# Filling TensorE's gaps at the start of a fused FFN, attention and FFN kernel, and reordering its first transfers and copies

## The chip, the cores and the metric

The kernel runs on one core of one Trainium2 chip. The time is the device time of the whole program in microseconds (us). The kernel before the change took 918.1 us, the median of three runs (916.91 to 918.52).

## The reference, cut to what matters

x has 8 batches of 512 rows of 256 numbers, all in fp32. The two FFNs share their weights. Their butterflies are linear maps of 1,024 features in 10 stages, where stage s pairs features 2^s apart.

```python
def _L0_ffn_ref(x, W_exp, b_exp, up_weights, up_bias, down_weights, W_con, b_con, down_bias):
    h = jnp.einsum('bsd,dh->bsh', x, W_exp) + b_exp
    h = butterfly(h, up_weights, D_HIDDEN)
    h = jax.nn.gelu(h + up_bias, approximate=False)
    h = butterfly(h, down_weights, D_HIDDEN)
    y = jnp.einsum('bsh,hd->bsd', h, W_con) + b_con
    return y + down_bias
...
x = x + 0.5 * ffn(layernorm(x))
x = x + attention(layernorm(x))   # causal, 16 heads, 32 numbers per head
x = x + 0.5 * ffn(layernorm(x))
```

## The kernel before, in words

Everything between x and the gelu is linear, and so is everything behind it, so the kernel first folds each butterfly into a dense matrix: W_exp and the up butterfly become `wup_sb` (256 x 1,024), W_con and the down butterfly become `wdn_sb`. This folding is the prologue, and it is where the change lies. After it, all eight batches run through FFN, attention and FFN with plain matrix products, in an order written out by hand (the `ORDER` strings), one token per step. There the engines' queues are fixed.

The prologue, in the order in which it is written (from L572):

- SyncE's queue issues the large loads: the up butterfly's tables `upe_sb` in two pieces (L117, L118), W_exp in two halves of 4 blocks (L120), the first x (`load_x(0)`, L106), the tables of the down butterfly, W_con, the second x, the attention weights, two more x. ScalarE's queue issues five small ones (L121 to L125), among them `upc_sb`, the coefficients of the high stages, and the two biases.
- GpSimd makes the identity (`ident`), the causal mask and constants.
- `low_matrices` (L208, VectorE) multiplies the tables of the seven low stages into one 128 x 128 matrix for each of the 8 blocks of 128 features. VectorE then adds the two output biases and halves them (`bhalf`).
- `low_up` (L237, TensorE) multiplies W_exp with these matrices: eight products of 128 x 257, into eight PSUM banks: four of the tile `low_up`, three of pool `ps_a` (`low_up_0` to `_2`), one of `ps_o`. Pool `ps_a` has three banks in all, and all later tiles `pxt`, `pup`, `ph`, `low_dn` turn in it.
- `ln_stats` and `ln_apply` normalize the first x. The statistics are VectorE's (L152 to L154), the rstd GpSimd's (L156). For this first x GpSimd also does the normalization (L167), and behind each half of it the addition of `bhalf` to x (L172), which is the residual with the biases already in it. VectorE does the normalization of all other x.
- Three high stages (`high_stage`, L221 and L226) combine blocks that are 1, 2 and 4 apart. For each block ScalarE scales it (`mine`), and VectorE adds the partner, scaled. The first stage reads PSUM, the other two read SBUF.
- Behind the second stage, the normalized x is transposed by TensorE (L180, `pxt`, four transposes for each half of the 256 columns) and copied from PSUM by VectorE (L181).
- `finish_up` transposes the result of the third stage (L246, `pup`, 16 transposes in four quarters), copied to `wup_sb` by ScalarE and VectorE in turn (L247). GpSimd adds the bias column (L241).
- Layer one of the first x follows on TensorE (L271, `ph`, then gelu on ScalarE, L278), three of its eight steps between each two high stages of the down butterfly (`high_dn`), then `low_down` (L252) makes `wdn_sb`, and layer two follows (L289, `py`).

An fp32 product of TensorE stands in the trace as two records, each with its own weight load; a transpose stands as one.

## Time and profile before

| what | value |
|---|---|
| median of 3 runs | 918.1 us (916.91 to 918.52) |
| the profiled execution | 918.08 us |
| its span, first to last instruction | 916.3 us |
| mean granted TensorE clock | 0.987 |
| TensorE busy | 880.8 us (96%) |
| VectorE busy | 634.1 us (69%) |
| ScalarE busy | 495.9 us (54%) |
| GpSimd busy | 87.5 us (10%) |

The span is what the trace shows; 1.8 us of the profiled execution lie outside it. Times within it count from its first instruction. PE is TensorE, PEld its weight loads, DVE VectorE, ACT ScalarE, POOL GpSimd, SP SyncE. The end of a TensorE record is modelled, so where records follow closely, the distance between their starts says what one costs. The granted clock is the share of the full clock that TensorE is given.

In the first 30 us the large transfers land one after the other, each about 1.4 us after the one before: the first half of W_exp at 9.58, the second at 10.98, the first x at 12.43, the last x at 27.46.

### The profile page before, as it was taken

What the parts mean: (1) busy time and instruction counts of PE and PEld (TensorE: products, weight loads), DVE (VectorE), ACT (ScalarE), POOL (GpSimd) and SP (SyncE); (2) the same over time, 40 slices, a digit from 0 to 9 for tenths busy, and PEclk for the clock granted to TensorE, in tenths of its full rate; (3) what the DMA queues carried; (4) which work ended last, traced back from release to release, by engine and by line L of the source; (5) the groups of instructions that cost most, each with busy time, mean ns of one, the idle gap of its engine ahead of it and who ended that gap; (6) DMA issues with size and microseconds to landing.
All of it is one profiled execution on the core that took longest, in us unless ns stands there. A gap on an engine that the chain in (4) does not pass through costs nothing.

```text
span 916.3 us, 13349 instructions
## 1 busy us (share of the span) xinstructions
PE 880.8 (96%) x4464; PEld 516.3 (56%) x4464; DVE 634.1 (69%) x1772; ACT 495.9 (54%) x1336; POOL 87.5 (10%) x103
## 2 busy tenths in 40 slices
PE   3999999999999999999999999999999999998988
PEld 2474654666547465564746655465655554743746
DVE  5854986898619985399826987189767886987230
ACT  4615677646537455554736465356558367558111
POOL 4321000022000210012000220002100200010010
PEclk9799999999999999999999999999999999999989
DMA  9100555555651356542572555604554565665500
GB/s 328 52 1 1 127 127 127 127 127 127 150 149 41 88 138 161 127 118 63 137 181 56 127 126 127 172 18 110 139 146 120 133 152 144 160 175 145 150 1 23
DMA packets 37812, 108.14 MB, mean 118 GB/s; under 512 B 9200, under 2 KB 20208, under 8 KB 37744
## 3 DMA queue, kind: packets, MB, share of 16 engines
q1 hardware_dynamic: 37024, 106.98, 45.8%
q8 instruction: 35, 0.57, 0.3%
q10 hardware_dynamic: 720, 0.32, 0.1%
q14 instruction: 33, 0.27, 0.1%
HBM read 10.79 MB, written 4.19 MB: 16 GB/s over the span
## 4 chain that ended last, share of the span: by engine, by line
PE 92%; DVE 4%; DMA 1%; POOL 1%; issue 1%; ACT 1%; DVEq 0%; SPq 0%; POOLq 0%; ACTq 0%
PE ph_f L271 25%; PE py_f L289 25%; PE pp L314 12%; PE sc L364 10%; PE po L465 6%; PE pv L328 6%; PE pa L444 5%; DVE e L378 3%; PE pxt_f L180 2%; PE pxt_at L180 1%; DMA x<-in_x_dram 1%; POOL xn_f L167 1%; DMA upc_sb<-in_up_c_dram 0%; PE pup L246 0%; ACT e L391 0%
## 5 line engine op out<-in xcount | busy, mean ns | idle before, releaser
L391 ACT ACTIVATE e<-e,nm 128x128 f32<-128x128 f32 (+3 forms) x512 | 280.2, 549 | 108.9 <-DVE nm L378 108.3
L378 DVE CUSTOM_DVE_ANT_0 e<-sc,mask 128x128 f32<-128x128 f32 (+3 forms) x512 | 216.3, 486 | 124.8 <-PE sc L364 124.7
L271 PE MATMUL ph_f<-xnt_f,wup_sb 128*128 128x512 f32 x512 | 234.6, 605 | 0.0
L289 PE MATMUL py_f<-wdn_sb,g_f 128*128 128x256 f32 x1024 | 233.2, 382 | 0.0
L289 PEld LDWEIGHTS py_f<-wdn_sb,g_f 128*128 128x128 f32 x1024 | 191.3, 190 | 35.3 <-issue 6.5
L409 DVE STREAM_TRANSPOSE pr<-e 128x1536 f32<-128x1536 f32 (+2 forms) x128 | 170.7, 1356 | 5.8 <-ACT e L391 5.8
L278 ACT ACTIVATE g_f<-ph_f,bup_sb 128x512 f32<-128x512 f32 x128 | 86.5, 686 | 150.7 <-PE ph_f L271 150.4
L271 PEld LDWEIGHTS ph_f<-xnt_f,wup_sb 128*128 128x128 f32 x512 | 97.4, 194 | 117.3 <-issue 106.9
L364 PE MATMUL sc<-kt,qt 32*128 32x128 f32 (+3 forms) x1024 | 91.9, 461 | 10.0 <-DVE nm L378 8.1
L391 ACT ACTIVATION_READ_ACCUMULATOR e<-e,nm 128x1 f32 x512 | 95.8, 187 | 0.0
L156 POOL TENSOR_TENSOR rstd_f<-mv_f,mhalf 128x2 f32<-128x2 f32 x32 | 22.5, 704 | 633.7 <-DVE mv_f L154 630.6
L444 PE MATMUL pa<-pt,v 128*32 128x512 f32 (+3 forms) x1024 | 75.5, 436 | 0.3 <-issue 0.2
L364 PEld LDWEIGHTS sc<-kt,qt 32*128 32x128 f32 x1024 | 44.6, 184 | 51.2 <-issue 21.5
L444 PEld LDWEIGHTS pa<-pt,v 128*32 128x32 f32 x1024 | 30.4, 110 | 60.0 <-issue 53.7
L314 PE MATMUL pp<-xnt_at,wq_sb 128*128 128x512 f32 x128 | 61.5, 603 | 0.0
L314 PE MATMUL pp<-xnt_at,wk_sb 128*128 128x512 f32 x128 | 60.7, 596 | 0.0
L465 PE MATMUL po<-wo_sb,ot 128*128 128x256 f32 x256 | 58.8, 382 | 0.0
L328 PE MATMUL pv<-wv_sb,xnt_at 128*128 128x512 f32 x128 | 57.7, 595 | 0.0
L451 DVE TENSOR_TENSOR ot<-pa,pt 128x512 f32<-128x512 f32 x32 | 21.8, 681 | 51.3 <-PE pa L444 50.3
L298 DVE SCALAR_TENSOR_TENSOR x<-py_f,x 128x512 f32<-128x512 f32 x32 | 21.7, 678 | 49.4 <-PE py_f L289 49.4
L465 PEld LDWEIGHTS po<-wo_sb,ot 128*128 128x128 f32 x256 | 48.1, 190 | 9.0 <-issue 2.2
L172 POOL TENSOR_TENSOR x<-x,bhalf 128x512 f32<-128x512 f32 x32 | 40.9, 1279 | 32.9 <-DVE xn_f L167 32.2
(69 smaller groups left out, 578.1 us busy)
## 6 DMA issues: line engine op xcount, KB each, us to landing
pt<-pr SPq DMA_DIRECT2D x512, 176.0 KB, 4.0
x<-in_x_dram SPq DMA_DIRECT2D x8, 512.0 KB, 5.5
out_dram<-x SPq DMA_DIRECT2D x16, 256.0 KB, 3.8
wexp_sb<-in_wexp_t_dram SPq DMA_DIRECT2D x2, 514.0 KB, 6.9
wcon_sb<-in_wcon_dram SPq DMA_DIRECT2D x1, 1024.0 KB, 9.1
dne_sb<-in_dn_e_dram SPq DMA_DIRECT2D x1, 1016.0 KB, 7.2
upe_sb<-in_up_e_dram SPq DMA_DIRECT2D x1, 512.0 KB, 6.3
wq_sb<-in_wq_dram SPq DMA_DIRECT2D x1, 512.0 KB, 10.4
```

The lines of the kernel that those rows point to most:

```text
L172: nc.gpsimd.tensor_tensor(x2, x2, bhalf.rearrange("p (o c) -> p o c", o=1).to_broadcast([P, 2, C]), ALU.add)
L271: nc.tensor.matmul(ph[:, :N], lhsT=wup_sb[:, kc, bass.ts(fc, P)], rhs=xnt[:, kc, :], start=(kc == 0), stop=(kc == KC - 1),)
L278: nc.scalar.activation(g[:, fc, :], ph[:, :N], AF.Gelu, bias=bup_sb[:, fc : fc + 1])
L289: nc.tensor.matmul(py[:, i, :], lhsT=g[:, fc, bass.ts(t, P)], rhs=wdn_sb[:, fc, :], start=(fc == 0), stop=(fc == NBLK - 1),)
L314: nc.tensor.matmul(pp[:, :N], lhsT=w[:, kc, bass.ts(g, P)], rhs=xnt[:, kc, :], start=(kc == 0), stop=(kc == KC - 1))
L328: nc.tensor.matmul(pp, lhsT=xnt[:, kc, bass.ts(t, P)], rhs=wv_sb[:, kc, :], start=(kc == 0), stop=(kc == KC - 1))
L364: nc.tensor.matmul(sc[:, j, at : at + n], lhsT=kept["q", b, gg][r, bass.ts(qb, P)], rhs=kept["k", b, gg][r, :n], start=(i == 0), stop=True ...
L378: nc.vector.tensor_tensor_reduce(out=e[:, j, at : at + n], in0=sc[:, j, at : at + n], in1=mask[:, N - n :], scale=-1.0, scalar=3.0e38, op0 ...
L391: nc.scalar.activation(e[:, j, at : at + n], e[:, j, at : at + n], AF.Exp, scale=-1.0, bias=nm[:, qb, gg, j : j + 1], accum_out=zs[:, gg, ...
L409: nc.vector.transpose(pr[:, :, :, qb : qb + 3 * n - 2 : 3, :].rearrange("p j h k r -> p h k j r"), blocks[:, :, :n])
L444: nc.tensor.matmul(by_row[r, :, kb * 32 :], lhsT=v[:, kb, bass.ds(g * P + j * HD, HD)], rhs=pt[:, :, bass.ds(j * NSLOT + SLOT[kb] + kb, NT ...
L465: nc.tensor.matmul(po[:, i, :], lhsT=ot[:, g, bass.ts(t, P)], rhs=wo_sb[:, g, :], start=(g == 0), stop=(g == NG - 1))
```

## The change

- `load_x(0)` is issued between the two halves of W_exp and no longer behind both.
- For the normalization on GpSimd (the first x alone) the two additions of `bhalf` are no longer done behind each half; they are a function of their own, `ffn_bias`, called behind the high stages. On GpSimd's queue they come directly behind the four normalizations.
- The transposes of the first normalized x and their copies move from behind the second high stage to behind the third, and the copies from VectorE to ScalarE.
- A new function, `keep_busy`, multiplies the identity with itself into a PSUM tile that nothing reads: 50 times at the very start, in the bank that `low_up_o` gets later, and 12 times between the transposes of x and those of W_up, in bank 6 of `ps_a`.

In the built program's queues, TensorE has the 50 products, then the eight of `low_up`, eight transposes of x, the 12 products, and from there the order of before. The banks of `pxt`, `pup` and `ph` stay the same; the first quarter's `pup` takes over the bank of the 12 products, and the second and third take those of `pxt`, which ScalarE's copies free. VectorE's queue loses the two copies, and ScalarE's has them between its last `mine` of the third stage and the first copy of `pup`.

```diff
     for blocks in (slice(0, NBLK // 2), slice(NBLK // 2, NBLK)):
         nc.sync.dma_start(out=wexp_sb[:, blocks, :], in_=wexp_t.rearrange("(n p) c -> p n c", p=P)[:, blocks, :])
+        if blocks.start == 0:
+            load_x(0)
...
-    load_x(0)
     nc.sync.dma_start(out=dne_sb, in_=dn_e)
...
-        if what != "at":
-
-            nc.gpsimd.tensor_tensor(
-                x2, x2, bhalf.rearrange("p (o c) -> p o c", o=1).to_broadcast([P, 2, C]), ALU.add
-            )
-
-    def transposed(b, what, xn, xnt, kc):
+        if what != "at" and engine is nc.vector:
+            ffn_bias(b, half)
+
+    def ffn_bias(b, half):
+
+        x2 = xt[b][:, 2 * half : 2 * half + 2, :]
+        nc.gpsimd.tensor_tensor(x2, x2, bhalf.rearrange("p (o c) -> p o c", o=1).to_broadcast([P, 2, C]), ALU.add)
+
+    def transposed(b, what, xn, xnt, kc, copy=nc.vector.tensor_copy):
...
-        nc.vector.tensor_copy(xnt[:, kc, :], pt[:, :N])
+        copy(xnt[:, kc, :], pt[:, :N])
...
+    def keep_busy(pool, tag, times):
+
+        idle = pool.tile([P, 512], F32, name=f"idle_{times}", tag=tag)
+        for _ in range(times):
+            nc.tensor.matmul(idle[:, :P], lhsT=ident, rhs=ident, start=True, stop=True)
+
...
     with fold, tc.manual_schedule():
+        keep_busy(ps_o, "pa", 50)
         mats = low_matrices(upe_sb, "up")
...
         for i in range(HIGH):
             cur, whole = high_stage(cur, i, upc_sb, "up", C + 1, NBLK)
-            if i == 1:
-                run(ln_steps(0, "f1"))
+        run(ln_steps(0, "f1", copy=nc.scalar.copy), partial(ffn_bias, 0, 0), partial(ffn_bias, 0, 1))
+        keep_busy(ps_a, "a", 12)
         finish_up(cur, whole)
```

## The prediction

> **What bounds the kernel now.** I read the page first, then the chain of waits for the first 75 us, then the timelines of TensorE and VectorE there, then the windows of the clock. On the page TensorE is busy in 96% of the span, and its idle slices lie at both ends:

> ```profile
> PE   3999999999999999999999999999999999998988
> PEclk9799999999999999999999999999999999999989
> ```

> One slice is 22.9 us. The change touches only the first two. From 30.2 us on TensorE is dense up to 821 us, in a written order, so whatever moves the first product of layer one (L271, 30.20) or its clock moves the end by as much; nothing else here can. The chain of waits in order of time (start, length, what):

> ```profile
> 5.48 6.95 DMA x<-in_x_dram
> ...
> 15.88 2.41 POOL xn_f L167 x2
> 18.37 1.51 POOL x L172
> 19.88 3.75 POOL xn_f L167 x2
> ...
> 23.67 1.34 PE pxt_f L180 x5
> ...
> 25.65 0.49 DVE high_up L226
> ...
> 26.18 4.22 PE pup L246 x16
> 30.40 14.89 PE ph_f L271 x32
> ```

> First x lands at 12.43; GpSimd normalizes it, with a bias addition in between; TensorE transposes it; VectorE copies it and only then does its last high stage. VectorE's timeline shows the price of that place (start, length, count, idle before):

> ```profile
> 18.27 4.42 DVE L226 SCALAR_TENSOR_TENSOR high_up<-high_up,upc_sb,mine_up 128x257 f32<-128x257 f32 x8
> 24.19 0.69 DVE L181 COPY xnt_f<-pxt_f 128x512 f32<-128x512 f32 x1 [1.50 <-PE pxt_f L180]
> 25.04 0.69 DVE L181 COPY xnt_f<-pxt_f 128x512 f32<-128x512 f32 x1 [0.16 <-PE pxt_f L180]
> 25.65 3.25 DVE L226 SCALAR_TENSOR_TENSOR high_up<-high_up,upc_sb,mine_up 128x257 f32<-128x257 f32 x8
> ```

> The second stage ends at 22.69, the third starts at 25.65: 2.96 us of waits and copies. The second stage itself takes 4.42 for eight, the third 3.25: one of its instructions lasts 1.50 instead of 0.48, beside GpSimd's bias addition (18.37, 1.51).

> The clock needs two views. TensorE's timeline:

> ```profile
> 9.72 6.14 PE L237 MATMUL low_up<-wexp_sb,mat_up 128*128 128x257 f32 x14 [9.72 <-DMA wexp_sb<-in_wexp_t_dram]
> 15.69 0.60 PE L237 MATMUL low_up_o<-wexp_sb,mat_up 128*128 128x257 f32 x2
> ```

> Fourteen records in 6.14 us start 0.43 us apart; the last two, 0.22. So the clock was at half speed until about 15.5, though the granted-clock column shows 1.00 there: it knows nothing before its first event. From then on it can be read (window, length, PE, PEld, DVE, ACT, POOL, clock, DMA):

> ```profile
> 15.53:18.94 3.41, 1.39 (x6) 0.61 (x4) 3.41 (x10) 3.34 (x9) 3.33 (x4) 1.00 1.08 393
> ...
> 25.77:29.18 3.41, 3.00 (x12) 2.34 (x13) 3.41 (x9) 0.59 (x1) 0.20 (x1) 0.50 0.16 52
> 29.18:32.60 3.42, 3.42 (x9) 2.03 (x8) 2.34 (x7) 3.01 (x8) 0.00 (x1) 0.50 0.00 0
> 32.60:36.01 3.41, 3.41 (x9) 1.52 (x8) 3.38 (x7) 3.32 (x5) 0.00 (x0) 1.00 0.02 5
> 824.48:827.90 3.42, 1.80 (x18) 0.80 (x11) 3.12 (x8) 2.06 (x9) 0.00 (x0) 1.00 0.58 138
> 838.14:841.55 3.41, 1.16 (x17) 0.81 (x17) 2.19 (x8) 2.96 (x6) 0.00 (x0) 1.00 0.99 264
> ```

> All changes lie on one grid of 3.41 us. A window with 1.39 or 1.16 us of TensorE work is followed by half clock, one with 1.80 is not; a window full of work is followed by full clock. Half clock costs layer one (32.6 - 30.2) / 2 = 1.2 us today.

> **The change, part by part.** All times below are of the profiled execution (918.08 us, 1.8 outside its span); it stands at the median of the runs, 918.1.

> *Fifty products of the identity.* They begin when GpSimd has made it (1.61), say at 1.8. Each fp32 product is two records (the fp32 products of L289 are 1024 records for 512). The trace has no 128-column ordinary stream, so from both sides: by columns, L289's 256-column record every 0.216 us gives 0.108; the 128-column transposes start 0.11 apart at full and 0.21 at half clock (L246); weight loads of 128 columns start 0.11 apart at best (82.67 and 82.78). Above, one load is recorded as 0.19, which would hold only if loads were not hidden, and beside L289 they are. I take 0.109 and 0.214: 10.9 us at full speed, 21.4 at half. When does the clock rise? The rows say 5.8 us after dense work began (9.7 to 15.5) and 6.4 (26.2 to 32.6, with gaps at first). [...] Half-speed records by then: (6.9 - 1.8) / 0.214 = 24; the other 76 take 8.3; the fifty end at 15.2 (14.4 to 16.0).

> That is late. low_up stands behind them on TensorE, and began at 9.72. Now it begins at 15.2, at full clock: its first four blocks, eight records, are done 1.9 us later instead of 3.7; ScalarE's first product (13.52 before) starts at 17.1, and VectorE's first stage 0.45 later, 17.6 instead of 15.13. It loses 2.45 us.

> *x between the halves of W_exp.* The two transfers swap: x lands at 10.98, the second half at 12.43 instead of 10.98 (both have 0.5 MB, queues are full). Statistics end 1.4 us earlier, at 13.7. This gains nothing while low_up ends them later; the swapped half is hidden by the fifty, and would cost up to 1 us without them, as blocks 4 to 7 would wait to 12.4. The transfers after them keep their places on SP; ScalarE's queue is not touched.

> *Biases behind, copies to ScalarE.* GpSimd runs rstd, then four normalizations without the addition: 14.5 + 4 x 1.21 = 19.3 instead of 23.6, beside a first stage that reads PSUM and did not slow it before. The additions follow at 19.3 and 20.6, to 21.9, and meet the second stage, which starts about 20.7; the sum for bup_sb behind them on GpSimd waits for the third stage anyway. Cost as seen: 1.0 (0.3 to 1.2), against 1.25 before. VectorE loses both copies and their waits: 2.96 gained. ScalarE's 24 products end 0.55 after the second stage, at 25.4, and it idled 4.6 us there; two copies of 0.59 end at 26.6, well before layer one. Behind them in its queue stand the W_up copies, and the transposes of the second and third quarter wait for the banks that the copies free (26.0 and 26.6): they are due at 26.6 and 27.0, so nothing.

> Sum for the end of the third stage: 28.90 + 2.45 - 2.96 - 0.2 = 28.2 (27.1 to 28.2 over the phases, since an early rise brings low_up forward). TensorE then needs 1.2 us of transposes at half clock, or 0.75, the copy of the second quarter, at full clock. Layer one starts at 28.3 to 29.3 instead of 30.20: 1.3 us, on the mean.

> *Twelve products.* The transposes of x run at 19.4 to 20.3, the twelve (24 records, 2.6 us) wait for bank 6, free after the first stage (20.6), and end at 23.2; behind them stand the W_up transposes, not due before 25.3. The first W_up transpose comes at 25.3, and until 28 they come at VectorE's pace, 0.4 us apart. So there is again a hole of 2.1 us and sparse work after it. With the grid at its four phases I get a window under 1.4 us of work, hence half clock, in about two of four; in the other two the clock survives and the 1.2 us are saved. Where it falls, a window of transposes and layer one must raise it. Rows: the window 29.18 to 32.60 was full, a third of it transposes, and did. [...] I take the row. Mean saving on the clock 0.6 to 0.7.

> Total: -1.3 - 0.65 = -1.9 us: 916.2. By phase the same sum runs from -2.7 to -1.2.

> **Rivals.**
> *A, the fifty end before W_exp is there*, if an identity product costs half of what I take. For: nothing but that the trace has no such row. Then low_up starts at 9.7, waits for the second half to 12.4, statistics decide (13.7), the third stage ends near 24.7, layer one starts at 25.5, warm: -4.7 - 1 = about 912.5.
> *B, slower: the identity stream does not raise the clock.* Place: in front of low_up. The fifty then take 21.4 us, to 23.2; low_up at half clock brings the first stage to 27.3, the third to 36.8, layer one to 38: +8, 926. Loss begins when the fifty end after 16.9 (28.9 - 11.9), which is a rise after 10.4 us. Against: low_up raised it within 5.8 us, and the stream is as dense; for: the operands are nearly all zeros, and no row has such.
> [...]

> **How the numbers follow.** My forecast 0.64, A 0.12, B 0.05, C 0.16, and 0.03 for a loss that I do not see. A difference under 0.2%, 1.8 us, cannot be told from none here. Of the forecast's phases some six in ten lie beyond -1.8 (0.39), the rest within. Faster: 0.39 + 0.12 = 0.51; same: 0.25 + 0.15 = 0.40; slower 0.09. The range takes in A's 912.5 and C with a bad phase, 919: 912.4 to 919.2; outside are B and the unseen loss.

> **What would show it.** The fifty ending at 14.4 to 16.0 and low_up's records 0.22 apart; ScalarE's first product near 17; no copy between the second and third stage, third stage ending at 27 to 28.2; layer one at 28.3 to 29.3; half clock, if at all, only between about 25.7 and 31. Wrong if the fifty end before 12 or after 17, if bias additions cost VectorE over 1.5 us, or if half clock lasts past 32.

## The result and the profile after

| | before | changed |
|---|---|---|
| median of 14 runs each | 918.12 us (916.74 to 921.70) | 918.13 us (916.34 to 921.16) |
| profiled execution, span | 918.08, 916.3 | 916.75, 915.0 |
| mean granted clock in it | 0.987 | 0.996 |

The ratio of the runs is 1.0001, 95% interval 0.9989 to 1.0013: no difference that can be measured. Yet the profiled execution is 1.3 us shorter, and its page shows what the change was meant to do: TensorE is busy from the start, and its clock row is full at both ends.

```profile
PE   8999999999999999999999999999999999998988
PEclk9999999999999999999999999999999999999999
```

To see where time went I cut each trace at two points that every kernel here has: the first product of layer two of the first batch, and the first score of the last batch. I call the three pieces head, middle and end.

| profile | layer one starts | head | middle | end | half clock at (number of 3.41 us windows) |
|---|---|---|---|---|---|
| before | 30.20 | 48.77 | 722.74 | 144.77 | 18.9 (4), 841.6 (1), 879.1 (2) |
| changed | 29.31 | 47.23 | 722.74 | 144.99 | 825.9 (1), 880.5 (1) |

The change gained 1.54 us in the head; the end took 0.22 longer, and the remaining 1.3 us is what this execution's span is shorter by. The chain of waits of the changed kernel (start, length, what) is a different one from before; x, GpSimd's normalization and the copies have left it:

```profile
1.67 13.82 PE idle L247 x100
15.49 1.76 PE low_up L240 x8
...
17.27 1.58 ACT mine_up L224 x4
...
18.88 1.50 DVE high_up L229 x4
...
25.39 3.27 DVE high_up L229 x8
...
28.70 0.34 PE pup L255
...
32.87 1.28 ACT L287
...
34.16 0.70 ACT g_f L287
...
34.90 8.85 PE ph_f L280 x20
```

Line by line: the hundred records of the identity now hold TensorE to 15.49, and `low_up` waits for them, not for W_exp. VectorE's first stage follows the *fourth* of ScalarE's products (17.27 + 1.58 = 18.85). The later stages run without a break. And a link appears that the prediction had not named: ScalarE's table load and first gelu, which stand in its queue behind eight products for the down butterfly (29.55 to 32.85), and on which layer one waits until 34.90. VectorE's timeline (start, length, count, idle before) shows that the copies are gone from between the stages, and that the second and third together now take 6.62 us:

```profile
18.88 2.44 DVE L229 SCALAR_TENSOR_TENSOR high_up<-low_up,upc_sb,mine_up 128x257 f32<-128x257 f32 x6 [5.03 <-ACT mine_up L224]
...
22.03 6.62 DVE L229 SCALAR_TENSOR_TENSOR high_up<-high_up,upc_sb,mine_up 128x257 f32<-128x257 f32 x16
28.57 0.68 DVE L256 COPY wup_sb<-pup 128x512 f32<-128x512 f32 x1
```

TensorE's timeline shows the twelve products between the transposes, those of W_up at full clock (3.45 us where before had 4.22), and the new wait:

```profile
22.16 2.94 PE L247 MATMUL idle<-ident 128*128 128x128 f32 x24
26.02 3.45 PE L255 MATMUL pup<-ident,high_up 128*128 128x128 f32 x16 [0.91 <-DVE high_up L229]
29.31 5.42 PE L280 MATMUL ph_f<-xnt_f,wup_sb 128*128 128x512 f32 x12
34.90 8.85 PE L280 MATMUL ph_f<-xnt_f,wup_sb 128*128 128x512 f32 x20 [0.18 <-ACT g_f L287]
```

So two questions are left. Is the head's gain what the prediction thought it was, and which part of the change makes it? And why do the medians not show it?

### The profile page after: what moved, and what is told of

Read it like the earlier page. It is cut to its first block, busy times and chain, and to the rows that moved or that the text cites. A ratio compares the mean times of both kernels' runs of the same rounds, so it can differ in the third digit from the quotient of the medians.

```text
span 915.0 us, 13597 instructions
## 1 busy us (share of the span) xinstructions
PE 890.5 (97%) x4588; PEld 527.2 (58%) x4588; DVE 632.1 (69%) x1770; ACT 496.6 (54%) x1338; POOL 85.8 (9%) x103
## 4 chain that ended last, share of the span: by engine, by line
PE 92%; DVE 5%; ACT 1%; issue 1%; DVEq 0%; POOL 0%; POOLq 0%
PE py_f L298 25%; PE ph_f L280 24%; PE pp L323 12%; PE sc L373 10%; PE po L474 6%; PE pv L337 6%; PE pa L453 5%; DVE e L387 3%; PE pxt_f L183 2%; PE idle L247 2%; DVE high_up L229 1%; PE pxt_at L183 1%; ACT e L400 0%; PE low_dn L261 0%; ACT mine_dn L224 0%
## 5 line engine op out<-in xcount | busy, mean ns | idle before, releaser
L307 DVE SCALAR_TENSOR_TENSOR x<-py_f,x 128x512 f32<-128x512 f32 x32 | 21.7, 678 | 48.4 <-PE py_f L298 48.4
```

## The experiments

Two theories on the head. The **queue theory**: the order of x, biases and copies gains, and the fifty take part of it back, because `low_up` stands behind them. Its rival: the fifty pay for themselves, through the full clock. Every kernel below computes everything that the reference does; only unread products are added or taken away, or the order changes. Each ratio is to runs of the kernel before on the same chip (35, 37 or 33 of them, with medians of 917.84, 917.48 and 917.65 us on the three chips used); it is taken over the runs and is not simply the quotient of the two medians. All times that are read off come from one profile each. The head of the changed kernel was 47.23, 47.36 and 47.26 in three profiles, and in these three the clock rose at nearly the same time, 6.7 to 7.0. Where the clock's phase differs, a head differs more: that of the kernel before took 48.77 in its own profile and 48.20 in that of the kernel with the end filled (below), with full clock from 32.6 and from 31.4. So a difference of less than some 0.6 us between two heads can be the phase alone.

### Fewer products at the start, none, and none at all

```diff
-        keep_busy(ps_o, "pa", 50)
+        keep_busy(ps_o, "pa", 20)
```

> The changed kernel with 20 instead of 50 products of the identity at the start. Queue theory (the fifty end at 15.5 and hold low_up back by 5.8 us; that eats the gain of the reordering): the twenty end by about 8.6, low_up starts at 9.6 to 9.8, VectorE's first stage starts at about 14 behind the statistics, not 18.9; the third stage ends near 25, layer one starts at 25.5 to 28; median 913 to 916. Rival, clock theory (when low_up starts does not matter; the time is made by how long the clock is at half speed, and a shorter stream loses it sooner): layer one starts no earlier than 29 and median 918 to 920.5.

Measured: a median of 918.31 us (916.49 to 920.64), ratio 1.0000 (0.9987 to 1.0012). `low_up` began at 9.95 at full clock and the third stage ended at 25.8, both as the queue theory has it. Layer one did not follow: it started at 29.63, past what was expected. TensorE's timeline says why:

```profile
22.46 5.23 PE L247 MATMUL idle<-ident 128*128 128x128 f32 x24
27.74 2.00 PE L255 MATMUL pup<-ident,high_up 128*128 128x128 f32 x16
29.63 14.38 PE L280 MATMUL ph_f<-xnt_f,wup_sb 128*128 128x512 f32 x32
```

The transposes of W_up were ready at 25.8, and the twelve products stood in front of them until 27.7. They were late because they come behind the transposes of x, whose normalization GpSimd did beside VectorE's second stage:

```profile
14.68 6.61 POOL L168 TENSOR_SCALAR xn_f<-x,mv_f,rstd_f 128x256 f32<-128x256 f32 x4
```

That is 6.61 us, against 4.83 for the same four in the changed kernel. And they were at half clock (5.23 us where they take 2.94 in the changed kernel), since TensorE had been nearly idle since 14.8. Products meant to keep the clock had become the wait.

The fifty left out, the twelve kept:

```diff
-        keep_busy(ps_o, "pa", 50)
```

> The changed kernel without the first 50 products, with the 12 later ones. Queue theory: low_up starts at 9.7 at half clock, VectorE's first stage at about 14, third stage ends near 25; but the twelve then run at half clock in most executions (24 records of 0.214, 5.1 us, from about 20) and stand in front of the transposes of W_up, so layer one starts at 26 to 29: median 914.5 to 917. Clock theory: as slow as the slowest runs of the changed kernel, 920 or more.

Measured: 918.54 us (915.19 to 920.37), ratio 0.9991 (0.9976 to 1.0007). Layer one at 27.90, head 45.84: 1.4 us better than with the fifty. But the runs fell into two groups, six from 915.2 to 915.7 and eight from 918.5 to 920.4, with nothing between. I come back to that.

Neither of them, only the order:

```diff
-        keep_busy(ps_o, "pa", 50)
...
-        keep_busy(ps_a, "a", 12)
```

> The changed kernel without any product of the identity: the earlier x, the additions behind and the copies on ScalarE alone. Queue theory: third stage ends near 25 against 28.8 before, layer one starts at about 26, at half clock until 29 to 31: median 913.5 to 915.5, so faster than the full change. Clock theory: no gain beyond what the whole change has, 917.5 to 919, since the clock is at half speed as long as before.

Measured: 917.21 us (915.49 to 920.25), ratio 0.9994 (0.9981 to 1.0007). Head 46.71: in the head the order alone gains 2.06 us, more than the whole change. (The medians of the two do not differ beyond the scatter of the runs.) VectorE's timeline:

```profile
15.07 2.45 DVE L229 SCALAR_TENSOR_TENSOR high_up<-low_up,upc_sb,mine_up 128x257 f32<-128x257 f32 x6 [1.32 <-ACT mine_up L224]
...
18.21 8.98 DVE L229 SCALAR_TENSOR_TENSOR high_up<-high_up,upc_sb,mine_up 128x257 f32<-128x257 f32 x16
```

The first stage is 3.81 us earlier than in the changed kernel (15.07 against 18.88), but the two stages after it take 8.98 instead of 6.62, because now they meet GpSimd's bias additions. Two of VectorE's sixteen instructions make nearly all of the difference: they start at 19.64 and 21.16 and take 1.60 and 1.48 us where the others take 0.48, and GpSimd's timeline has its two bias additions there:

```profile
19.68 2.68 POOL L177 TENSOR_TENSOR x<-x,bhalf 128x512 f32<-128x512 f32 x2
```

So of the 3.8 us that the fifty cost, 2.4 come back: they delay the stages past GpSimd's additions. In TensorE's timeline the transposes of W_up are at half clock again:

```profile
24.48 4.22 PE L255 MATMUL pup<-ident,high_up 128*128 128x128 f32 x16 [3.50 <-DVE high_up L229]
28.49 14.73 PE L280 MATMUL ph_f<-xnt_f,wup_sb 128*128 128x512 f32 x32
```

### The twelve left out, and the products alone

```diff
-        keep_busy(ps_a, "a", 12)
```

> The changed kernel without the 12 later products; the 50 stay. Third stage ends at 28.6 as with them. If the 12 keep the clock (the change's purpose), TensorE now idles from 22 to 26 and the clock falls in most executions: layer one at half speed for some us, first product of layer two at 48 to 49.5 instead of 47.2. If they are not needed or stand in the way, 47.2 as before.

Measured: 919.55 us (919.21 to 921.96), ratio 1.0027 (1.0018 to 1.0036). The clock fell from 24.1 to 30.9, and TensorE's timeline has the half-clock transposes again:

```profile
26.07 4.23 PE L255 MATMUL pup<-ident,high_up 128*128 128x128 f32 x16 [3.77 <-DVE high_up L229]
30.10 14.32 PE L280 MATMUL ph_f<-xnt_f,wup_sb 128*128 128x512 f32 x32
```

Head 47.89, 0.66 us more. `low_up` itself began 0.16 later here (15.48 against 15.32), so the twelve are worth about 0.5 us in the head of this profile: they hold the clock through the hole. The runs are slower by more than that; in the profile the rest lies in the end, which took 146.8 us (below).

The kernel before with all 62 products, each at the place that the change gives it (the twelve stand behind the third stage), and nothing else:

```diff
     with fold, tc.manual_schedule():
+        keep_busy(ps_o, "pa", 50)
...
+        keep_busy(ps_a, "a", 12)
         finish_up(cur, whole)
```

> The kernel before with only the products of the identity added (50 at the start, 12 in front of the transposes of W_up); x, additions and copies as before. Queue theory: low_up starts at 15.5 and VectorE's first stage at 18.9 instead of 15.13, third stage ends near 30 instead of 28.8 (the wait for x's normalization between the stages becomes shorter), layer one starts at 30.6 or later, at full clock if it survives: first product of layer two at 48.5 to 50 against 48.77 before, median 918 to 919.5. Clock theory: full clock saves its 1.2 us and more: first product of layer two at 47.5 or earlier.

Measured: 919.58 us (917.61 to 923.71), ratio 1.0021 (1.0011 to 1.0032): a small loss. The profile has a head of 48.30, 0.47 us under before, which can be the phase alone, and it is of the fastest of the 18 runs. The clock rose early in it, at 4.7 against 6.7 in the changed kernel, so that `low_up`, which is on this kernel's chain too, started at 14.38 and not at 15.3. With a later rise the gain would be gone (an estimate from this one profile); what the slower runs lost, and where, no profile shows. TensorE's timeline:

```profile
14.38 3.21 PE L237 MATMUL low_up<-wexp_sb,mat_up 128*128 128x257 f32 x14
...
23.10 3.85 PE L244 MATMUL idle<-ident 128*128 128x128 f32 x24
```

### Products where they hold nothing up

Twenty at the start, 26 between `low_up` and the transposes of x, and no twelve in front of W_up's:

```diff
-        keep_busy(ps_o, "pa", 50)
+        keep_busy(ps_o, "pa", 20)
...
+        keep_busy(ps_a, "a", 26)
         run(ln_steps(0, "f1", copy=nc.scalar.copy), partial(ffn_bias, 0, 0), partial(ffn_bias, 0, 1))
-        keep_busy(ps_a, "a", 12)
```

> The changed kernel with 20 products at the start, 26 between low_up and the transposes of x, and none between those and the transposes of W_up. Queue theory: TensorE's products then stand only in front of work that is not due. low_up starts near 9.9, VectorE's first stage at 13.8, third stage ends near 25.8 (as with 20 and 12); the 26 run from about 16 to 22 at full clock, the transposes of x behind them to 23; layer one starts at 26.3 to 27 at full clock, the first product of layer two at 44 to 45 (48.8 before, 47.2 changed). The end of the program adds its own scatter of up to 3.4 us; median 913 to 915.5. Rival (the clock alone sets the time, and it was already full in the changed kernel's profile): first product of layer two at 47, median as the changed kernel.

Measured: 917.05 us (913.93 to 918.91), ratio 0.9989 (0.9975 to 1.0003). TensorE's timeline:

```profile
9.78 1.98 PE L240 MATMUL low_up<-wexp_sb,mat_up 128*128 128x257 f32 x8 [0.64 <-DMA wexp_sb<-in_wexp_t_dram]
...
15.66 6.07 PE L247 MATMUL idle<-ident 128*128 128x128 f32 x52 [1.16 <-DVE high_up L229]
...
26.20 5.42 PE L280 MATMUL ph_f<-xnt_f,wup_sb 128*128 128x512 f32 x12
```

Head 44.13, at full clock from 7.5 us on: 4.64 us under before and 3.10 under the changed kernel. The queue theory stands. But the median moved by 0.4 us only, inside its interval. This can't be explained from the head of this profile.

### The end

All ten profiles up to here have the same middle, 722.72 to 722.80 us. What differs is the end: 144.8 to 145.05 in seven, 146.8 in one, 148.3 in two, and one of those two is the kernel with the shortest head. The clock windows of the profile without the fifty (window, length, PE, PEld, DVE, ACT, POOL, clock, DMA) show it:

```profile
825.42:828.84 3.42, 3.42 (x11) 0.68 (x13) 3.42 (x13) 3.42 (x15) 0.00 (x0) 0.50 0.00 0
839.08:842.50 3.42, 3.07 (x18) 1.76 (x19) 1.21 (x7) 3.02 (x9) 0.00 (x0) 0.50 1.03 237
842.50:845.90 3.40, 3.40 (x6) 1.33 (x5) 3.40 (x13) 3.40 (x15) 0.00 (x0) 0.50 0.70 167
880.05:883.46 3.41, 2.16 (x7) 1.61 (x8) 2.68 (x4) 0.00 (x0) 2.31 (x2) 0.50 0.00 0
```

The last batch has no other batch to fill in for it, so TensorE has gaps at about 820, 837 and 877 (in the changed kernel 1.05 and 1.92 us idle at the first, 2.65 at the second, 2.60 at the third). The windows lie on a grid of 3.41 us, and where it lies against the gaps differs between the profiles: a window begins 0.84 us behind the score that ends the first idle stretch here (822.00, 821.16), and 0.04 us ahead of the same score in the changed kernel (822.48, 822.52). The same view of the changed kernel, two windows and their successors:

```profile
822.48:825.90 3.42, 1.47 (x17) 0.73 (x18) 2.88 (x3) 2.61 (x11) 0.00 (x0) 1.00 0.78 183
825.90:829.31 3.41, 3.41 (x4) 0.98 (x4) 3.38 (x17) 2.85 (x11) 0.00 (x0) 0.50 0.02 5
836.14:839.55 3.41, 2.04 (x11) 0.45 (x9) 1.30 (x5) 1.21 (x2) 0.00 (x0) 1.00 0.94 263
839.55:842.96 3.41, 2.13 (x19) 1.29 (x20) 2.14 (x10) 3.40 (x8) 0.00 (x0) 1.00 1.03 240
```

The first has 1.47 us of TensorE work and is followed by half clock; the third has 2.04 and is not. (Where a row is at half clock its PE time is stretched, as the identity's records are, 0.213 us apart there and 0.111 at full clock, so only rows at 1.00 are compared.) In the kernel without the fifty the grid lay so that the window at the second gap, from 835.67, had only 1.10 us of work: half clock from 839.08 to 845.90, and after the third gap two windows of it instead of one. Its 148.35 us of end gave back the head.

The runs themselves say how often this happens, since each comes with its mean clock. The 14 of the changed kernel: five from 916.3 to 917.1 at 0.996, four from 918.0 to 918.5 at 0.993, five from 920.3 to 921.2 at 0.987 to 0.991. (Two windows of half clock in 915 us make a mean of 0.996, six make 0.989.) Two more profiles of it were taken to find the upper groups:

> The changed kernel once more, for a profile of another execution; nothing is altered. Its times fall in groups (916.3 to 917.0, 918.0 to 918.5, 920.3 to 921.2). If this one is of the last group, the queue theory with the clock's grid expects: half clock falls between the end of low_up and the transposes of x, and the 12 products run at half clock (24 records 0.214 apart, 5.1 us) in front of the transposes of W_up, so layer one starts after 31. If it is of the first, layer one starts at 29.3 as in the profile at hand.

> The changed kernel once more, for a profile of a further execution. The middle of the program (first product of layer two of the first x to the last batch's first score product) took 722.7 to 722.8 in every profile so far. If the three groups of its times come from the program's end, the start will again be 47.2 to 47.4 and the end 145 or 148; if they come from the start, this one's first product of layer two is at 47.3 or at 49 to 51.

Measured: 916.75 and 916.81 us, ends of 144.84 and 145.05, windows of half clock at the same places. All three profiles of the changed kernel are of the lowest group, so the other groups are known by their clock alone, which does not say where in the program it was lost.

The test of it is to fill the gaps. The same edit went into three kernels: 4 and 6 unread products ahead of the scores of unit 7 and between its halves, 8 ahead of unit 9, 8 ahead of the last transposes of x, in the bank of `pa`.

```diff
-... t5 q+0 t6b u7 g-1 t6a t7a p1 2g-1 m2 g-1 u8 u9 ...
+... t5 q+0 t6b k4 u7 g-1 t6a t7a p1 2g-1 m2 g-1 u8 k8 u9 ...
...
+            if i and b == B - 1 and (kind, g) == UNITS[7]:
+                keep_busy(ps_o, "pa", 6)
...
         run([partial(ln_apply, last, "f2", half) for half in range(2)])
+        keep_busy(ps_o, "pa", 8)
         run(ln_steps(last, "f2"))
```

> The kernel before, with 26 unread products of the identity in four idle stretches of TensorE in the last batch and nowhere else: 4 ahead of the scores of unit 7, 6 between its two halves, 8 ahead of unit 9, 8 ahead of the last transposes of x. Theory of the end (the scatter of 3 to 4 us among the runs comes from windows of 3.41 us in which the sparse last batch leaves TensorE under about 1.5 us of work): the end from the first score of the last batch on takes 142.5 to 144.0 us in the profile (144.77 without the products), no half clock after 815, the runs lie within about 1.5 us of each other, and the median falls to 914.5 to 916.8. Rival (the scatter arises elsewhere, and products in the gaps only stand in front of the scores): end 144.8 or longer, runs as scattered as before, median 918 to 919.5.

> The changed kernel with the same 26 unread products in the last batch. If the change does gain about 1.5 us in the head and the end alone hid it, this kernel stands 1.2 to 1.8 us under the kernel before with the same products (913.0 to 915.3 where that one is at 914.5 to 916.8), with the runs of each within about 1.5 us. If the head's gain is taken back between head and end by something that follows it (rival), the two kernels have the same median within 0.5 us although both ends are at full clock.

> Twenty products first and 26 between the first stages and the transposes of x, no twelve (head 4.6 us shorter than before), with the same 26 unread products in the last batch. Theory of the end: head about 44.1, end 142.5 to 144.0, median 910.5 to 912.8, which is 2.8 to 3.4 us under the changed kernel with the same products, and every run within about 1.5 us. Rival: end 147 to 148.3 as in the profile without the products, median 916 to 917.5.

| kernel, end filled | runs | median | ratio to the kernel before, end not filled | head, end in the profile |
|---|---|---|---|---|
| before | 13 | 917.65 (916.07 to 918.26) | 0.9993 (0.9980 to 1.0005) | 48.20, 144.44 |
| changed | 21 | 916.37 (914.67 to 917.34) | 0.9982 (0.9974 to 0.9990) | 47.01, 144.09 |
| twenty and 26 | 5 | 913.37 (913.22 to 913.59) | 0.9948 (0.9931 to 0.9966) | 44.13, 144.72 |

The long runs are gone. Of 33 runs of the plain kernel before on the same chip four were above 920, of these 39 none; the changed kernel had five of 14 above 920, and has none of 21 with the end filled, where its code differs at the end alone (the 14 may have run on another chip). And with the ends alike the heads come through: the changed kernel stands 1.28 us under before (0.40 to 1.71, resampling the runs of both), for 1.19 between their heads (the clock rose at 5.5 in the changed kernel's profile); the last one 3.00 under the changed kernel (2.62 to 3.41), for 2.88. The last is the fastest of all kernels here, 4.3 us under before.

One part of what I expected failed: the end did not shrink to 142.5 to 144, the median of before did not fall, and the runs of the first two kernels spread over 2.2 and 2.7 us, not 1.5. TensorE's timeline of the kernel before with its end filled:

```profile
822.27 1.05 PE L246 MATMUL idle<-ident 128*128 128x128 f32 x8
...
824.13 1.60 PE L246 MATMUL idle<-ident 128*128 128x128 f32 x12
...
840.89 5.42 PE L279 MATMUL ph_f<-xnt_f,wup_sb 128*128 128x512 f32 x12
848.19 2.36 PE L454 MATMUL pa<-pt,v 128*32 128x512 f32 x32 [1.88 <-DMA pt<-pr]
```

The products of L279 (L271 in the plain kernel) take 5.42 us here and 7.11 at half clock there, but then `pa` waits 1.88 us for a transfer. In the plain kernel `pa` started at 848.72, without such a wait: the 1.69 us that one window of half clock cost there were hidden by the transfer. Two windows at that place, without the fifty, stood in a profile with an end of 148.35. Filling takes away the bad ends; it does not better the good ones. (One window behind the last eight products stayed at half clock in all three kernels' profiles, from 877.9, 879.3 and 881.3.)

### The wait for four products

The changed kernel's first stage starts with the end of ScalarE's fourth product. To see why, the instructions of all high stages were written block by block, each engine's own queue unchanged:

```diff
             if blk < on_scalar:
                 nc.scalar.activation(mine[blk], cur[blk], AF.Copy, scale=w_self)
             else:
                 nc.gpsimd.tensor_scalar(mine[blk], cur[blk], w_self, 1.0, ALU.mult, ALU.mult)
-        for blk in range(NBLK):
             w_other = coef[:, i, blk, 1:2]
             nc.vector.scalar_tensor_tensor(new[:, blk, :], cur[blk ^ (1 << i)], w_other, mine[blk], ALU.mult, ALU.add)
```

> The changed kernel, with the order of a high stage's instructions written block by block: ScalarE's product of a block, then VectorE's addition of that block, and no longer eight products and then eight additions. Only the waits change; each engine's own queue stays as it is. It asks why VectorE's first stage in the changed kernel begins at 18.88, with the end of ScalarE's fourth product, and not 0.45 us after the first began (17.27). Theory (the readers of one PSUM tile take turns in the order written, and the first four blocks lie in one tile, low_up): VectorE begins at about 17.75, but ScalarE's second product then waits for VectorE's first addition and so on, so that the additions of the first four blocks start 0.8 to 1.0 us apart instead of 0.39; the first stage ends at 23.5 to 25.5 instead of 22.1, and layer one starts at 30.5 to 32.5. Rival (the wait for four is only several waits drawn together, and nothing takes turns): VectorE begins at 17.75 and its additions stay 0.39 apart, the first stage ends at about 21.0, layer one starts at 28.0 to 28.5.

Measured, in one run: 919.81 us, head 50.17, layer one at 32.29. VectorE's timeline, then ScalarE's:

```profile
18.02 0.49 DVE L228 SCALAR_TENSOR_TENSOR high_up<-low_up,upc_sb,mine_up 128x257 f32<-128x257 f32 x1 [4.21 <-ACT mine_up L224]
19.05 0.49 DVE L228 SCALAR_TENSOR_TENSOR high_up<-low_up,upc_sb,mine_up 128x257 f32<-128x257 f32 x1 [0.55 <-ACT mine_up L224]
```

```profile
17.50 0.48 ACT L224 ACTIVATE mine_up<-low_up,upc_sb 128x257 f32<-128x257 f32 x1 [11.36 <-PE low_up L239]
18.54 0.48 ACT L224 ACTIVATE mine_up<-low_up,upc_sb 128x257 f32<-128x257 f32 x1 [0.56 <-DVE high_up L228]
```

Each engine waits for the other's reading of the same tile, and the additions start 1.03 us apart instead of 0.39. So in this program the readers of one PSUM tile take turns in the order written; `low_up` holds four blocks in one tile, and eight products written ahead of the eight additions make VectorE wait for four. The two later stages, which read SBUF, were written block by block too and show no such turns: their sixteen additions took 6.64 us, as in the changed kernel (6.62). The first stage ended at 24.4 instead of 22.1, as expected of the theory.

## Why the prediction was right, and where it was not

- **The fifty** end at 15.49, in the range of 14.4 to 16.0, 15.2 forecast; the records are 0.213 us apart at half and 0.111 at full clock (0.214 and 0.109 taken), the clock rises at 6.7 (6.9 taken). No run shows the 6.9 that was taken, nor the spread of it behind 14.4 to 16.0; the runs showed a rise at 6.7 to 7.0 in three profiles of the changed kernel, and between 4.7 and 7.5 in the other kernels that begin with this stream. That the time taken was so near is luck. That the identity's products do raise the clock rules out rival B; that they take as long as thought rules out rival A.
- **x between the halves of W_exp** landed at 11.18 and the second half at 12.66, each 0.2 us after the forecast, and both long before they were needed. **ScalarE's first product** at 17.27, forecast 17.1. Right.
- **The first stage, "0.45 later, 17.6"**: this step failed. It began at 18.88. The addition waits for four products, 1.6 us, and not for one. In the kernel before this was hidden by a coincidence: there the fourth product (14.61, 0.49 us) and VectorE's statistics both ended at 15.10, and VectorE came to the stage at 15.13 without a wait. I priced the wait by a row in which it did not show; ScalarE's first product at 13.52 and the stage at 15.13 lay 1.6 us apart there too.
- **The bias additions, 1.0 us on VectorE**: nothing, for the first error's sake. The second stage began at 22.03, when GpSimd had finished the additions at 21.92. With an earlier first stage the term is real, and larger than forecast: without the fifty the two stages take 8.98 us, 2.36 more, of which 2.1 stand in the two instructions beside the bias additions.
- **The copies, 2.96 gained**: there is no gap between the stages now. Right. The third stage ends at 28.65, where 28.2 was forecast. That this is so close is in part luck: the first stage started 1.3 us later than forecast, and the two stages behind it saved 0.85 us more (4.0 against 2.96 + 0.2, since the additions cost nothing).
- **Layer one** at 29.31, on the edge of 28.3 to 29.3: 0.89 us gained where 1.3 was forecast. **The clock** in the head stayed full from 6.7 on, one of the phases reckoned with, for which 1.2 us were forecast. Of these 0.43 went into a new wait: at full clock TensorE's first twelve records of layer one were done before ScalarE's table load and first gelu (to 34.86). I had asked what is late next on the way to layer one, and not behind it. Measured are 0.65 us (1.54 less 0.89). That 0.65 was forecast too is luck: the forecast was a mean over phases of which half lose the clock, and no run shows what such a loss was taken to cost in that mean. The one profile with half clock in the hole, that without the twelve (24.1 to 30.9), showed about 0.5 us.
- The sum was 1.95 us for the head, and it measured 1.54, or 1.19 between the two kernels with their ends filled. **The time, 916.2**, was nearly met by the profiled execution (916.75) and not by the median of the runs, 918.13, which shows none of the 1.9 us. The stated range, 912.4 to 919.2, does hold it, but by luck: its upper part stood for a clock lost in the head (rival C, below, and a bad phase), and not for what happened. The failed step here is the first part's sentence that from 30.2 us on whatever moves layer one moves the end by as much. It holds for the middle, to 0.1 us. It does not for the last 100 us, whose own clock makes up to 3.6 us of difference between profiles. The prediction quoted two windows of just that stretch, 1.80 and 1.16 us of TensorE work, as a gauge for the clock, and did not ask what another phase of the grid would make of the end itself. With the gaps filled, the head's gain is in the medians.
- **Rival C**, at 0.16 the likeliest of the rivals, is the gain of the start given back to a clock that is lost in the hole and that W_up's transposes do not raise. It did not happen in any of the three profiles of the changed kernel, so the question whether transposes can raise the clock, on which I took the row of the window from 29.18 to 32.60, did not come up there. Leaving the twelve out loses the clock in the hole, half clock from 24.1 to 30.9, at about 0.5 us; and there the row was right, as the last section shows.

What stays open: the changed kernel had five of 14 runs above 920, the kernel before 16 of 119 over all its series of runs (one of 14, seven of 35, four of 37, four of 33). Whether its head, 1.5 us shorter, puts the end at a worse place of the grid, or this is chance, was not settled; no profile shows the upper group. Why the kernel with the products alone is slower than before, at a higher mean clock (0.993 in most of its runs), stays open too. And some 2.7 us between the runs of the changed kernel with filled end (914.67 to 917.34, nearly all at a clock of 0.998) have another cause than the clock.

## What to carry to other kernels

Unread products on a queue are work like any other (with twenty at the start, the twelve held W_up's transposes from 25.8 to 27.7): count what stands behind them when they end later than planned, and put them in front of work that is not yet due, not in front of work that is ready. A gain at the start need not reach the median: here 1.54 us of head moved it by 0.01 us, and 1.19 us of head stood beside 1.28 us of median once the end was filled. Where a sparse stretch at the end can keep or lose its clock, as this one did (half clock behind a window with 1.47 us of TensorE work, none behind one with 2.04), look at the mean clock of every run beside its time before the change is judged, and fill that stretch first. And an engine that is seen never to wait for another may simply have come late (VectorE at 15.13 in the kernel before, where the product it needed had ended at 15.10): price its wait from the other engine's rows.

## What was not expected of the hardware

```profile
21.17:24.58 3.41, 2.33 (x21) 2.12 (x21) 3.41 (x4) 1.51 (x4) 2.49 (x2) 1.00 1.07 357
24.58:27.99 3.41, 3.28 (x14) 1.74 (x13) 3.05 (x9) 2.41 (x6) 0.20 (x1) 1.00 0.56 178
874.49:877.90 3.41, 1.80 (x9) 0.99 (x10) 2.73 (x5) 0.00 (x0) 2.85 (x3) 1.00 0.00 0
877.90:881.31 3.41, 3.41 (x5) 1.34 (x6) 0.41 (x1) 0.00 (x0) 0.05 (x1) 0.50 0.00 0
```

  In the first, only 0.56 of the 2.33 us were other products than transposes (the 26 end at 21.7), and the clock stayed, where 1.47 us of ordinary products (changed kernel, 822.48) did not hold it: in this window the transposes counted. In the third, 1.80 us, all but 0.13 of it transposes, lost the clock, where the kernel before had kept it with 1.80 us of ordinary products; but 1.62 us of ordinary products (without the fifty, 822.00) had lost it too, so whether transposes count for less is not shown.

  For raising it, first the kernel without the twelve, then the kernel with twenty and 26 and its end not filled:

```profile
27.51:30.93 3.42, 3.42 (x14) 2.91 (x14) 2.48 (x6) 2.28 (x6) 0.20 (x1) 0.50 0.00 1
30.93:34.34 3.41, 3.41 (x9) 1.52 (x8) 3.24 (x8) 3.39 (x7) 0.00 (x0) 1.00 0.02 5
836.89:840.31 3.42, 2.65 (x17) 1.72 (x18) 1.21 (x7) 3.17 (x9) 0.00 (x0) 0.50 1.05 241
840.31:843.72 3.41, 3.41 (x5) 1.35 (x4) 3.41 (x17) 3.25 (x13) 0.00 (x0) 0.50 0.82 195
```

  The first of these windows was full and the clock rose behind it, though all but its last 0.83 us (layer one starts at 30.10) were transposes; in the third, 2.65 us of ordinary products did not raise it. So in the first the transposes helped to raise the clock.
- A stream of products of the identity, nearly all zeros, raised the clock 5.0 us after its start in the changed kernel, and in 3.1 to 5.8 us in the seven other kernels that begin with one. The products of `low_up`, in the four kernels without such a stream, took 3.1 to 5.8 us as well, so nothing shows that the zeros matter.
- Where GpSimd and VectorE ran beside each other, now the one took longer and now the other. With twenty products at the start, two of GpSimd's four normalizations ran beside VectorE's second stage and took 2.07 and 2.14 us instead of 1.22 (6.61 us for the four, 4.83 in the changed kernel), while VectorE's additions beside these two kept to 0.48, with one of 0.62. Beside the bias additions it was VectorE that was held: 1.60 and 1.48 us instead of 0.48 with the order alone, 1.55 and 1.50 with the twenty.
